# Two graph layers on one core: the run table of attention 1 as an input, its places sought ahead of the table of features, counts from the first gathered block on

## The chip, the cores and the metric

The kernel runs on one core of a Trainium2 chip. The metric is device time in microseconds; smaller is better. The program has five engines that work side by side: TensorE (PE, matrix products, with its weight loads as PEld), VectorE (DVE), ScalarE (ACT), GpSimd (POOL) and SyncE (SP, used here as a DMA queue). Each takes its instructions in the order of its own queue and waits for the others by semaphores. DMAs are issued from the queues of SP, ACT and POOL; a gather by indices (an indirect DMA) is issued from POOL.

## The reference

Two layers over a graph of 6250 nodes and 200,000 edges sorted by destination. The first is a graph attention of two rounds, the second a convolution over edges with a small network for each edge. Only the first round of attention and what it needs is touched by the change.

```python
def gat_layer(x, W, attn_l, attn_r, bias, src, dst, num_nodes):
    H, D = attn_l.shape
    feat = (x @ W).reshape(num_nodes, H, D)
    el = jnp.sum(feat * attn_l[None], axis=-1)
    er = jnp.sum(feat * attn_r[None], axis=-1)
    e = jax.nn.leaky_relu(el[src] + er[dst], NEG_SLOPE)
    m = jax.ops.segment_max(e, dst, num_segments=num_nodes)
    ee = jnp.exp(e - m[dst])
    s = jax.ops.segment_sum(ee, dst, num_segments=num_nodes)
    alpha = ee / s[dst]
    msg = feat[src] * alpha[:, :, None]
    rst = jax.ops.segment_sum(msg, dst, num_segments=num_nodes)
    return rst + bias.reshape(1, H, D)

h = jnp.maximum(_layernorm(x, axis=-1), 0.0)
h = gat_layer(h, W1, al1, ar1, b1, src, dst, N_NODES)   # 4 heads of 16
h = jax.nn.elu(h.reshape(N_NODES, -1))
h = gat_layer(h, W2, al2, ar2, b2, src, dst, N_NODES)   # 1 head of 128
x = x + h[:, 0, :]
# second layer: h = relu(layernorm(x)); messages over the edges from
# h[src], edge_attr_4 and two gelu layers of edge_attr_8; summed by dst
```

## The kernel before

The nodes are 49 blocks of 128 (`NB`); a block's edges are contiguous, since they are sorted by destination, and are read as a window of 34 tiles of 128 edges (`K`, `CAP`). The work has four stages.

**Preparation.** `x` is loaded in chunks of eight blocks by turns on the ACT and SP queues (`load_x`, L147 to L152). Both edge lists are loaded as 125 rows of 1600 (`di` and `si`, L168 to L175). From `di` come: the first edge of each block (L206 to L241, with one small indirect load `part_i`, L218), flags whether the list falls anywhere (`falls`, L201), and the low seven bits of each destination, written to `dlow` (L251 to L255). `features` in all but name is the loop at L574 to L602: layer norm statistics on VectorE (L291, L292), the normed and clipped block on ScalarE (L579), four transposes on TensorE copied out by VectorE (L312, L314), the product with the weights and attention vectors (L591), copied out by ScalarE (`t1`, L593) and VectorE (`er1`, L594); in four pieces it is written to HBM as `table1` (L597 to L600). The statistics come in two halves of 24 and 25 blocks. `node_factors` and `split3` make the factors of the destination nodes (`pq`, `pq3`), `widely` checks a spread (L441 to L452). Last, for each of 3136 half-block windows of 64 sources, ten comparisons with every 160th destination (L620) and 250 small products (L622) give the segment where its run of edges begins (`wseg`).

**Attention 1.** Two methods run side by side. Blocks 0 to 32 (`NG = NB - DENSE1` = 33) are gathered: for each of 34 tiles POOL gathers 128 rows of `table1` by source (L319, into `G`, six buffers of eight tiles), and `attend` makes weights and messages on VectorE (L324, L362 to L367), halves them (L331, L332), and sums them into nodes on TensorE (L377). `finish1` closes four blocks at a time and writes what attention 2 reads (`rhs2d`, L830). Blocks 33 to 48 are dense: `dense1` yields 128 steps (8 passes of 14 steps, a start and an end), each of which loads counts of edges between all sources and four destination blocks (L861), makes a ramp on ScalarE (L892), takes a minimum on VectorE (L895) and sums on TensorE (L902, L908); a pass ends with L915 to L943. These counts, which attention 2 needs for all 49 blocks, are made by `count` in 196 steps (four per block): VectorE compares slots with a cut list of edges (L773, twice), TensorE multiplies (L784), ScalarE copies out (L786), and a DMA on ACT's queue writes them (L788).

To cut the lists, `write_runs` writes a run table `runs` to HBM: row n holds sources and destinations of 128 edges from 16n on, as int16, in ten DMAs on ACT's queue during blocks 0 and 1. `seek_windows` finds each window's row in it: 25 indirect loads on POOL (`wpart_i`, L715), each followed by a comparison and a sum on VectorE (L720, L721). `fetch_run` gathers 128 rows of the run table (L731, 25 times) and `cut_windows` turns them into keys (L740 to L756). `fill_rhs1` turns `table1` into the dense method's right sides, seven calls (L694 to L705).

The order is written out by hand in the loop over `b` and the groups `q` (8, 8, 8, 8 and 2 tiles): each group issues its gathers and then as many counting and dense steps as are due. Counting starts at block `LAG` = 3, dense at block `LAG_D` = 7, and both are due in full with the last tile of block 32. `step` issues the second part of a step after the first part of the next. VectorE and TensorE mostly follow this order, but a planner may put an instruction ahead of others unless it is kept in program order (`keep`).

**Attention 2** begins after a branch that all engines meet at, and is dense for all blocks; **the convolution** follows. Neither is changed in its instructions.

Of the kernel before, what the change touches and what calls it, by code (L numbers as in the profile page):

```python
# [53 lines left out]
LAG = 3  # L54
AHEAD = 4
DENSE1, LAG_D = 16, 7
# [10 lines left out]
def gnn_kernel(ctx: ExitStack, tc: tile.TileContext, x, src, dst, attr4, attr8,  # L67
               W1, al1, ar1, b1, W2, al2, ar2, b2,
               Wl0, Wl1, Ws0, Ws1, Wm1, Wm2, Wtp, Wf0, Wf1, src_t, dst_t, attr4_t, attr8_t, out):
# [23 lines left out]
    NROW = (E - WCAP) // WSTEP + 1  # L93
# [11 lines left out]
    ps_bank = ps_pre.enter_context(tc.tile_pool(name="ps_bank", bufs=2, space=PSUM))  # L105

# [52 lines left out]
    fin = one.enter_context(tc.tile_pool(name="fin1", bufs=1))  # L159
    aw = one.enter_context(tc.tile_pool(name="aw", bufs=2))  # L160
# [3 lines left out]
    df = seek.enter_context(tc.tile_pool(name="df", bufs=1)).tile([GP, ROWT + 1], F32, name="df")  # L164
    listed = ExitStack()
    find = listed.enter_context(tc.tile_pool(name="find", bufs=1))
    both = []
    for name, v in (("di", dst), ("si", src)):  # L168
        t = find.tile([GP, ROWT + WCAP], I32, name=name)
        nc.vector.memset(t[:, ROWT:], NB * P)  # L170
        rows = v.rearrange("(p t) -> p t", p=GP)
        nc.sync.dma_start(t[:, :ROWT], rows)
        nc.sync.dma_start(t[:GP - 1, ROWT:], rows[1:, :WCAP])
        both.insert(0, t)

    w1_sb = const.tile([D, HD], F32, name="w1_sb")
    nc.scalar.dma_start(w1_sb, W1)
    load_x()
    w2_sb = const.tile([HD, D], F32, name="w2_sb")
    nc.scalar.dma_start(w2_sb, W2)  # L180
    a1_sb = const.tile([HD, 2 * H1], F32, name="a1_sb")
    nc.vector.memset(a1_sb, 0.0)
    for j, a in ((0, al1), (1, ar1)):
        for h in range(H1):
            nc.scalar.dma_start(a1_sb[h * DH:(h + 1) * DH, j * H1 + h:j * H1 + h + 1],
                                a[h:h + 1, :].rearrange("o d -> d o"))
    a2_sb = const.tile([D, 2], F32, name="a2_sb")
    for j, a in ((0, al2), (1, ar2)):
        nc.scalar.dma_start(a2_sb[:, j:j + 1], a.rearrange("o d -> d o"))
# [5 lines left out]
    wfirst = const.tile([P, NC], I32, name="wfirst")  # L195

    runs = dram.tile([NROW, 2, WCAP], I16, name="runs")
    di = both[1]
    nc.vector.tensor_copy(df, di[:, :ROWT + 1])
    falls = find.tile([GP, ROWT], F32, tag="row", name="falls")  # L200
    nc.vector.tensor_tensor(falls, df[:, :ROWT], df[:, 1:], op=OP.is_gt)  # L201
    fall = find.tile([GP, 1], F32, name="fall")
    nc.vector.tensor_reduce(fall, falls, axis=AX.X, op=OP.max)
    NS = ROWT // SEG
    below = find.tile([GP, NB + 1, NS], F32, name="below")
    nc.vector.tensor_tensor(below, df[:, 0:ROWT:SEG][:, None, :].to_broadcast([GP, NB + 1, NS]),  # L206
                            starts[:GP, :, None].to_broadcast([GP, NB + 1, NS]), op=OP.is_lt)
    nbelow = find.tile([GP, NB + 1], F32, name="nbelow")
    nc.vector.tensor_reduce(nbelow, below, axis=AX.X, op=OP.add)
    ps = small()  # L210
    nc.tensor.matmul(ps[:NB + 1, 0:1], nbelow, ones[:GP], start=True, stop=True)
    nc.tensor.matmul(ps[:NB + 1, 1:2], fall.to_broadcast([GP, NB + 1]), ones[:GP], start=True, stop=True)
    seg = find.tile([NB + 1, 1], F32, name="seg")
    nc.vector.tensor_scalar(seg, ps[:NB + 1, 0:1], -1.0, 0.0, op0=OP.add, op1=OP.max)
    seg_i = find.tile([NB + 1, 1], I32, name="seg_i")
    nc.vector.tensor_copy(seg_i, seg)
    part_i = find.tile([NB + 1, SEG], I32, name="part_i")
    nc.gpsimd.indirect_dma_start(  # L218
        out=part_i, out_offset=None, in_=dst.rearrange("(s t) -> s t", t=SEG),
        in_offset=bass.IndirectOffsetOnAxis(ap=seg_i[:, 0:1], axis=0))  # L220
    part = find.tile([NB + 1, SEG], F32, name="part")
    nc.vector.tensor_copy(part, part_i)
    nc.vector.tensor_scalar(part, part, own_start[:NB + 1], None, op0=OP.is_lt)
    found = find.tile([NB + 1, 2], F32, name="found")
    nc.vector.tensor_reduce(found[:, 1:2], part, axis=AX.X, op=OP.add)
    nc.vector.scalar_tensor_tensor(found[:, 0:1], seg, float(SEG), found[:, 1:2], op0=OP.mult, op1=OP.add)
    nc.vector.tensor_copy(found[:, 1:2], ps[:NB + 1, 1:2])
    pr = small()
    for j in range(2):
        nc.tensor.matmul(pr[:1, j * P:j * P + NB + 1], found[:, j:j + 1], ident[:NB + 1, :NB + 1],  # L230
                         start=True, stop=True)
    ends = find.tile([1, 2, NB + 1], F32, name="ends")
    nc.vector.tensor_copy(ends, pr[:1, :2 * P].rearrange("o (j b) -> o j b", j=2)[:, :, :NB + 1])
    first = find.tile([1, NB], F32, name="first")
    nc.vector.tensor_scalar(first, ends[:, 0, :NB], float(E - CAP), None, op0=OP.min)
    nc.vector.tensor_copy(first_i, first)
    nc.vector.tensor_sub(over, ends[:, 0, 1:], first)
    nc.vector.tensor_scalar(over, over, float(CAP), None, op0=OP.is_gt)
    nc.vector.tensor_scalar(falls_at_all, ends[:, 1, :NB], 0.5, None, op0=OP.is_gt)
    nc.vector.tensor_tensor(over, over, falls_at_all, op=OP.max)  # L240
    nc.vector.tensor_sub(n_edges, ends[:, 0, 1:], ends[:, 0, :NB])  # L241


    raws = []
    LONG = max(ROWT + WCAP, HS * 4 * P)
    for t in both:
        raw = pool.tile([P, LONG], BF16, tag="row", name="raw", bufs=3)[:GP, :ROWT + WCAP].bitcast(I16)
        nc.scalar.copy(raw, t)
        raws.append(raw)
    low_i = find.tile([GP, ROWT], I32, tag="row", name="low_i")  # L250
    nc.vector.tensor_scalar(low_i, di[:, :ROWT], P - 1, None, op0=OP.bitwise_and)  # L251
    low = find.tile([GP, ROWT], BF16, name="low")
    nc.vector.tensor_copy(low, low_i)
    dlow = dram.tile([E], BF16, name="dlow")
    nc.sync.dma_start(dlow.rearrange("(p t) -> p t", p=GP), low)  # L255
    listed.close()

    def write_runs(i, n):

        per = ROWT // WSTEP  # L260
        j, i, n = i * 2 // n, i % (n // 2), n // 2
        ends = [(GP - 1) * i // n, (GP - 1) * (i + 1) // n]
        for p0, p1, m in [(*ends, per)] + [(GP - 1, GP, NROW - (GP - 1) * per)] * (i == n - 1):
            a = raws[j][p0:p1, :]
            nc.scalar.dma_start(
                runs[p0 * per:p0 * per + (p1 - p0) * m, j, :].rearrange("(p r) t -> p r t", r=m),
                bass.AP(tensor=a.tensor, offset=a.offset, ap=[a.ap[0], [WSTEP, m], [1, WCAP]]))
# [17 lines left out]
    def shift_window(b):  # L285
        nc.vector.tensor_scalar(dstw[:, b, :], raw_dst.pop(b), -float(b * P), None, op0=OP.add)
# [368 lines left out]
    for j in range(2):  # L655
        nc.scalar.dma_start(wm1_sb[j * NRAD:(j + 1) * NRAD, j * HID:(j + 1) * HID], Wm1)
# [891 lines left out]
```

## Time and profile before

| | us |
|---|---|
| three runs, median (lowest to highest) | 4396.92 (4395.07 to 4397.64) |
| the profiled execution | 4406.11 |
| its span | 4404.4 |
| first gather of attention 1 | 112.68 |
| last gather of attention 1 | 1777.59 |
| first load of attention 2 | 1845.50 |

| engine | busy us | share of the span |
|---|---|---|
| PE | 3042.9 | 69% |
| DVE | 3565.2 | 81% |
| ACT | 2712.6 | 62% |
| POOL | 2795.3 | 63% |

All three stages differ in their limits, so a share over the whole span says little about one of them. A line of a group names source line, engine, operation and tiles (written<-read), then busy time and the mean in ns of one, then the idle time of the engine just before these instructions and what ended it. "issue" is idle time for which the profile shows no cause. [...]

### The profile page before, as it was taken

The numbers are of one execution on the slowest core, as the hardware profiler recorded it, in microseconds if no ns is written. First come the engines' busy times: TensorE is split into PE (matmuls) and PEld (weight loads), VectorE is DVE, ScalarE is ACT, GpSimd is POOL, SyncE is SP. The second block draws the span as 40 slices with busy tenths as digits, with TensorE's granted clock in tenths as the row PEclk, the third lists the DMA queues.
The fourth block names the chain that finished last, engine by engine and source line by source line (L and its number), as shares of the span: only waits on it lengthen the run. The fifth ranks groups of instructions, "written<-read, shape, count | busy, mean of one in ns | idle before, by whom it ended". The sixth has DMA issues, their size and how long they took to land. (4 is left out here: it accounts for less than half of the span.)

```text
span 4404.4 us, 61759 instructions
## 1 busy us (share of the span) xinstructions
PE 3042.9 (69%) x19255; PEld 2147.9 (49%) x19256; DVE 3565.2 (81%) x6184; ACT 2712.6 (62%) x6200; POOL 2795.3 (63%) x2752
## 2 busy tenths in 40 slices
PE   4115665666477566579998677777777777777777
PEld 3115444544355444478887344444444444444444
DVE  5258776788688688688888799999999999899998
ACT  3024556576486577689999565555555555555555
POOL 0777777777777777110000777777777777777775
PEclk9999677677677778699999788888888888888888
DMA  4346464565466556554453222222222222222221
GB/s 109 67 120 171 128 168 129 164 177 158 126 178 165 150 156 169 172 177 167 153 171 107 61 63 63 62 63 64 62 63 63 63 62 63 63 62 63 64 61 51
DMA packets 410029, 484.00 MB, mean 110 GB/s; under 512 B 248457, under 2 KB 296367, under 8 KB 405454
## 3 DMA queue, kind: packets, MB, share of 16 engines
q1 hardware_dynamic: 258854, 239.58, 18.6%
q0 software_dynamic: 87952, 149.96, 15.0%
q10 hardware_dynamic: 62872, 90.28, 5.7%
q8 instruction: 159, 2.61, 0.3%
q14 instruction: 192, 1.57, 0.1%
HBM read 369.70 MB, written 109.82 MB: 109 GB/s over the span
## 5 line engine op out<-in xcount | busy, mean ns | idle before, releaser
L319 POOL DMA_INDIRECT G<-table,srcc x1563 | 1475.1, 944 | 1003.3 <-DVE kept L1239 525.6
L319 POOL DMA_INDIRECT G<-table,srcw x1122 | 1249.0, 1113 | 417.1 <-issue 314.9
L786 ACT CAST ca<-small 128x392 bf16<-128x392 f32 x784 | 350.2, 491 | 335.9 <-PE small L784 307.0
L892 ACT ACTIVATE up<-erb,sel 128x512 bf16<-128x512 f32 x784 | 516.1, 726 | 8.6 <-DMA oht<-dlow 3.6
L1188 ACT ACTIVATE ramp<-erb,sel 128x256 bf16<-128x256 f32 (+1 forms) x1225 | 491.7, 499 | 20.7 <-DVE up L1192 14.4
L1335 PE MATMUL whole<-halves,ohr 128*128 128x512 f32 x1563 | 503.9, 461 | 0.7 <-ACT acc L1365 0.7
L1277 ACT ACTIVATE g<-G,a 128x128 f32<-128x128 f32 x1563 | 481.4, 393 | 2.0 <-DMA G<-table,srcc 0.2
L1270 PEld LDWEIGHTS big<-wtp_sb,hid 64*128 64x128 f32 x3126 | 263.6, 249 | 372.8 <-issue 358.2
L1270 PE MATMUL big<-wtp_sb,hid 64*128 64x128 f32 x3126 | 306.1, 351 | 150.2 <-DVE halves L1324 149.8
L784 PE MATMUL small<-key,lo 128*128 128x98 bf16 x3136 | 299.9, 237 | 139.6 <-ACT ca L786 109.0
L908 PE MATMUL up<-up,rc 128*102 128x512 bf16 x784 | 297.0, 539 | 142.2 <-DVE up L895 141.4
L1335 PEld LDWEIGHTS whole<-halves,ohr 128*128 128x128 f32 x1563 | 316.6, 210 | 129.5 <-issue 54.1
L377 PE MATMUL whole<-halves,ohr 128*128 128x136 f32 x1122 | 240.1, 356 | 174.6 <-DVE halves L332 138.7
L1258 PE MATMUL layer<-hid,wm_sb 128*128 128x512 f32 x392 | 341.1, 969 | 11.9 <-ACT hid L1261 11.1
L1261 ACT ACTIVATE hid<-layer 128x512 f32<-128x512 f32 x392 | 230.8, 589 | 189.6 <-PE layer L1258 189.6
L1258 PE MATMUL layer<-a8t,wm_sb 16*128 16x512 f32 x392 | 230.0, 667 | 157.2 <-ACT hid L1261 148.1
L784 PEld LDWEIGHTS <-lo 128*128 128x128 bf16 x3136 | 228.7, 115 | 209.9 <-issue 175.9
L1315 ACT CAST halves<-mess 128x512 fp32r<-128x512 f32 x195 | 114.4, 587 | 329.7 <-DVE mess L1302 329.7
L1307 DVE TENSOR_TENSOR halves<-mess,halves 128x512 fp32r<-128x512 f32 x391 | 267.8, 685 | 55.3 <-ACT halves L1310 39.8
L377 PEld LDWEIGHTS whole<-halves,ohr 128*128 128x128 f32 x1122 | 204.7, 255 | 194.7 <-DVE halves L332 137.3
L1197 PE MATMUL big<-rhs,up 128*128 128x196 bf16 x2401 | 240.5, 250 | 49.6 <-DVE up L1192 41.6
L773 DVE TENSOR_TENSOR lo<-slots,turned 128x2048 bf16<-128x2048 bf16 x196 | 238.3, 1216 | 37.4 <-PE small L784 37.2
(296 smaller groups left out, 6294.4 us busy)
## 6 DMA issues: line engine op xcount, KB each, us to landing
counts<-ca ACTq DMA_DIRECT2D x196, 392.0 KB
ct<-counts SPq DMA_DIRECT2D x192, 392.0 KB
ctc<-counts SPq DMA_DIRECT2D x896, 56.0 KB
oht<-dlow SPq DMA_DIRECT2D x33, 1088.0 KB
G<-table,srcc POOLq DMA_INDIRECT x1563
rc<-rhs SPq DMA_DIRECT2D x56, 358.8 KB
G<-table,srcw POOLq DMA_INDIRECT x1122
a8t<-attr_rows SPq DMA_DIRECT2D x391, 16.0 KB
```

Of the source, the lines that this page charges most:

```text
L319: nc.gpsimd.indirect_dma_start(out=G[:, c, :], out_offset=None, in_=table, in_offset=bass.IndirectOffsetOnAxis(ap=idx[:, c:c + 1], axis=0))
L377: nc.tensor.matmul(acc, oh[:, c, :], ms[:, c].rearrange("e s f -> e (s f)"), start=start and c == 0, stop=stop and c == n - 1)
L784: nc.tensor.matmul(ps[:, k * NKEY:(k + 1) * NKEY], lo[:, a, :, r], ky[:, a, :, r], start=True, stop=True)
L786: nc.scalar.copy(ca[:, :, i * W:(i + WBANK) * W].rearrange("p h (k d) -> p h k d", d=W), ps[:, :WBANK * NKEY].rearrange("p (k h d) -> p h ...
L892: nc.scalar.activation(up[:, i], erb[:, j], AF.Relu, bias=sel1[:, h0 + i, 2 * q + j:2 * q + j + 1], scale=STEEP)
L908: nc.tensor.matmul(sums["ups"][j][:2 * C1, :], r[:, i, c:c + 2 * C1], up[:, i], start=h0 + i == 0, stop=h0 + i == NB - 1)
L1188: nc.scalar.activation(ramp[:, h, :n * P], erb[:, :n * P], AF.Relu, bias=sel2[:, h0 + h, :], scale=STEEP)
L1258: keep(nc.tensor.matmul(ph, w, x[:, :npr * P], start=True, stop=True))
L1270: keep(nc.tensor.matmul(pw[:, c, :], hid[half, j * P:(j + 1) * P], wtp_sb[half].rearrange("x p u -> x (p u)"), start=True, stop=True))
L1277: keep(nc.scalar.activation(g0[:, c], G[:, c, :], AF.Copy, scale=a0[:, c, :]))
L1307: keep(nc.vector.tensor_tensor(ms[:, cs, 1, 1], m, ms[:, cs, 0, 1], op=OP.subtract))
L1335: keep(nc.tensor.matmul(acc, oh[:, c, :], ms[:, c].rearrange("e s h i u -> e (s h i u)"), start=start, stop=stop))
```

## The change

The run table is laid out on the host and given as an input `runs`, int32 instead of int16; `si`, its int16 copies and `write_runs` go. Small weights that were put together from many DMAs come as whole inputs (`a1_w`, `a2_w`, `lin_w`, `wm1_w`, `wm2_w`, `wtp_w`, `wf_w`), mostly on SP's queue. The preparation is written out as pieces in an order that is kept: statistics in six parts (`stats`), features in five stages per four blocks (`features`, advanced together by `through`), with the transposes copied out by ScalarE, and the searches between them. The window search (`segments`, `fetch_parts`, `count_parts`, `window_rows`) now ends ahead of the loop. The pools `fin` and `aw` are opened after the preparation's pools close. In the loop counting starts at block 0 and is due three blocks before the end (`AFTER`); dense starts at block 4 and is due 20 tiles before the end (`AFTER_D`).

```diff
-LAG = 3
-DENSE1, LAG_D = 16, 7
+DENSE1, LAG_D, AFTER, AFTER_D = 16, 4, 3, 20
...
+    def segments(i0, i1):
+        for i in range(i0, i1):
+            below = find.tile([GP, NC * P], BF16, name="belowc", bufs=2)
+            keep(nc.vector.tensor_scalar(below, wstarts, df[:, i * WSEG:i * WSEG + 1], None, op0=OP.is_gt))
+            for c in range(NC):
+                keep(nc.tensor.matmul(pcount[:, c:c + 1], below[:, c * P:(c + 1) * P], ones_b, start=i + c == 0,
+                                      stop=i == NSEG - 1 and c == NC - 1))
...
+    def fetch_parts(q):
+        part = find.tile([P, NQS, WSEG], I32, name="wpart_i", bufs=2)
+        for j in range(NQS):
+            nc.gpsimd.indirect_dma_start(
+                out=part[:, j, :], out_offset=None, in_=dst.rearrange("(s t) -> s t", t=WSEG),
+                in_offset=bass.IndirectOffsetOnAxis(ap=wseg_i[:, q * NQS + j:q * NQS + j + 1], axis=0))
+        wparts[q] = part
+
+    def count_parts(q):
+        less = find.tile([P, NQS, WSEG], F32, name="wpart")
+        cs = slice(q * NQS, (q + 1) * NQS)
+        keep(nc.vector.tensor_tensor(less, wparts.pop(q), own_w[:, cs, None].to_broadcast([P, NQS, WSEG]), op=OP.is_lt))
+        keep(nc.vector.tensor_reduce(wfound[:, cs], less, axis=AX.X, op=OP.add))
...
+    def stats(i):
+        b0, n = 8 * i, 8 if i < NB // 8 - 1 else NB - 8 * i
+        mv = pre.tile([P, n, 2], F32, name=f"mv{i}")
+        for j in range(n):
+            norm_stats(mv[:, j, :], b0 + j)
+        c = coefs(b0, n, mv)
+        next(c)
+        return c
...
+        ht = work.tile([P, 4, P], F32, name="transp")
+        keep(nc.scalar.copy(ht[:, :len(hs), :], pt[:, :len(hs), :]))
...
+    def through(k):
+        for d in range(5):
+            if 0 <= k - d < len(gens):
+                next(gens[k - d])
+
+    c0 = stats(0)
+    keep(nc.vector.tensor_copy(df, di))
+    deque(c0, 0)
+    c1 = stats(1)
+    through(0)
+    segments(0, 1)
+    through(1)
...
+    segments(6, NSEG)
+    window_segments()
+    for q in range(2):
+        fetch_parts(q)
+    c3 = stats(3)
...
+    block_segments()
...
+    block_firsts()
+    deque(c4, 0)
+    c5 = stats(5)
+    through(8)
+    count_parts(0)
+    fetch_parts(2)
+    deque(c5, 0)
+    low_parts()
+    through(9)
+    write_table(0, 24)
...
+    through(16)
+    write_table(40, NB)
     pq = pool.tile([P, NB, 2 * H1], F32, name="pq")
     node_factors(pq, er1, H1)
     split3(pre, pq3, pq, [P, NB, 2 * H1])
+    for q in range(3, 5):
+        count_parts(q)
+    window_rows()
...
+    find_falls()
+    w2_sb, a2_sb = load_weights(("w2_sb", W2), ("a2_sb", a2_w))
...
     seek.close()
+    fin = one.enter_context(tc.tile_pool(name="fin1", bufs=1))
+    aw = one.enter_context(tc.tile_pool(name="aw", bufs=2))
...
-        run = cut.tile([P, 2, WCAP], I16, name="run", bufs=2)
+        run = cut.tile([P, 2, WCAP], I32, name="run", bufs=2)
...
     for b in range(AHEAD):
         load_window(b)
+    for c in chunks[:2]:
+        fetch_run(c)
     for b in range(AHEAD):
         shift_window(b)
     low = load_low(0)
+    tables[chunks[0]] = cut_windows(chunks[0])
     for b in range(NG):
-        if b == LAG - 1:
-            deque(seeking, 0)
-        if b == LAG:
-            tables[chunks[0]] = cut_windows(chunks[0])
...
-            if b < LAG - 1:
-                for _ in range(2):
-                    next(seeking, None)
-            if b + 1 < LAG:
-                write_runs(b * len(GROUPS) + q, (LAG - 1) * len(GROUPS))
-            if b == 1 or b == 2 and q < NB // HS - len(GROUPS):
-                fill_rhs1(((b - 1) * len(GROUPS) + q) * HS, HS)
...
-            due = len(steps) * ((b - LAG) * K + s + n) // ((NG - LAG) * K)
+            if b == 0 or b == 1 and q < NB // HS - len(GROUPS):
+                fill_rhs1((b * len(GROUPS) + q) * HS, HS)
+            due = min(len(steps), len(steps) * (b * K + s + n) // ((NG - AFTER) * K))
...
-            due = n_dense * ((b - LAG_D) * K + s + n) // ((NG - LAG_D) * K)
+            due = min(n_dense, n_dense * ((b - LAG_D) * K + s + n) // ((NG - LAG_D) * K - AFTER_D))
```

## The prediction

> **What bounds the kernel now.** I read the page's slices first, to see which engine is level where.
>
> ```profile
> span 4404.4 us, 61759 instructions
> ...
> DVE  5258776788688688688888799999999999899998
> ...
> POOL 0777777777777777110000777777777777777775
> ```
>
> One slice is 110 us. GpSimd (POOL) stands at 7 from the second slice to the sixteenth without a break, while VectorE (DVE) wanders between 2 and 8. That stretch is attention 1, so I cut it into windows: before the first gather, blocks 0 to 2, blocks 3 to 6, blocks 7 to 32, and what follows the last gather. The columns are PE, PE loads, DVE, ACT and POOL busy, with instruction counts, then the granted clock, DMA share and GB/s.
>
> ```profile
> 0.00:112.70 112.70, 49.09 (x422) 39.35 (x424) 62.93 (x215) 33.33 (x79) 7.43 (x17) 1.00 0.43 109
> 112.70:274.00 161.30, 19.29 (x134) 18.14 (x134) 46.76 (x150) 8.72 (x18) 121.68 (x126) 1.00 0.32 71
> 274.00:468.00 194.00, 97.05 (x743) 84.49 (x742) 156.17 (x395) 83.32 (x185) 148.44 (x146) 0.99 0.61 167
> 468.00:1778.50 1310.50, 844.09 (x5858) 608.64 (x5859) 1012.24 (x1784) 849.59 (x1689) 1028.56 (x902) 0.72 0.58 156
> 1778.50:1845.50 67.00, 38.28 (x240) 26.87 (x239) 43.25 (x117) 39.70 (x88) 0.03 (x1) 0.66 0.27 82
> ```
>
> POOL is idle ahead of the gathers and behind them. Is its 78% in between full? The groups of POOL between 112 and 1780 us, with the idle time before each and who ended it, answer that.
>
> ```profile
> L319 POOL DMA_INDIRECT G<-table,srcw x1122 | 1249.0, 1113 | 417.1 <-issue 314.9 <-PE pe L360 65.2 <-DMA G<-table,srcw 13.7
> L731 POOL DMA_INDIRECT run<-runs,wfirst x25 | 26.1, 1043 | 7.6 <-issue 7.0 <-DVE x L696 0.3 <-DVE far L750 0.3
> L715 POOL DMA_INDIRECT wpart_i<-in_dst,wseg_i x25 | 23.6, 945 | 7.6 <-issue 7.3 <-DMA G<-table,srcw 0.3
> ```
>
> Apart from the 65.2 us ahead of the first gather, the idle time is 0.3 us of issue per instruction. The table of waits shows the only real stop:
>
> ```profile
> POOL G L319 <- DVE msg L367: 13.2, 10, 7.5
> ```
>
> So POOL's queue is the path: 1249.0 + 351.9 (417.1 less 65.2) + 33.7 + 31.2 = 1665.8 us, exactly 112.7 to 1778.5. In that stretch the other engines matter only where they stop POOL. A gather takes 0.944 us undisturbed, 1.113 on average; the timeline shows what stretches it.
>
> ```profile
> 803.26 2.01 DVE L895 TENSOR_TENSOR up<-up,ctc 128x3584 bf16<-128x3584 bf16 x1
> 803.94 2.15 POOL L319 DMA_INDIRECT G<-table,srcw  x1 [0.30 <-issue]
> ...
> 809.78 1.23 DVE L773 TENSOR_TENSOR lo<-slots,turned 128x2048 bf16<-128x2048 bf16 x1 [0.46 <-PE small L784]
> 810.32 0.94 POOL L319 DMA_INDIRECT G<-table,srcw  x1 [0.31 <-issue]
> ```
>
> The dense minimum (L895, both operands in SBUF) holds a gather; the counting compare (L773, one operand in PSUM) does not. The start and the end of the stretch:
>
> ```profile
> 110.89 0.82 DVE L340 TENSOR_TENSOR pq<-rest,pq 128x392 bf16<-128x392 f32 x1
> ...
> 112.68 0.96 POOL L319 DMA_INDIRECT G<-table,srcw  x1 [65.17 <-PE pe L360]
> ...
> 1777.59 0.94 POOL L319 DMA_INDIRECT G<-table,srcw  x1 [0.30 <-issue]
> ...
> 1788.42 0.69 DVE L367 TENSOR_TENSOR msg<-G,msg 128x512 f32<-128x512 f32 x1
> ...
> 1820.69 0.23 DVE L990 TENSOR_TENSOR sums<-sums,whole 128x68 f32<-128x68 f32 x1 [3.76 <-ACT sums L989]
> ...
> 1841.04 0.70 DVE L829 TENSOR_TENSOR rr<-x,rr 128x520 bf16<-128x520 f32 x1
> ...
> 1845.50 0.34 ACTq L1169 DMA_DIRECT2D ct<-counts  x1
> ```
>
> The first gather starts when VectorE has finished its preparation; 67 us after the last one attention 2 begins. Lastly, VectorE's groups between 112 and 275 us: it sits idle behind the window search, in order, while counting hasn't begun.
>
> ```profile
> L720 DVE TENSOR_SCALAR wpart<-wpart_i,own_w 128x160 f32<-128x160 int32 x25 | 7.9, 315 | 63.3 <-DMA wpart_i<-in_dst,wseg_i 63.2
> ```
>
> **What the Trainium skill says.** *SBUF — State Buffer*, "Who interferes with whom": a VectorE instruction with two SBUF inputs contends with a GpSimd instruction that reads SBUF, and one in a two-port mode with any GpSimd instruction; the loser blocks. The trace agrees (2.15 us beside L895, 0.94 beside L773), although the page infers that descriptor generation escapes `tensor_tensor`. *DMA: Bandwidth & Descriptors*, "Anatomy of one DMA — SWDGE (gpsimd) path", gives about 2 us fixed from issue to completion; here the search of block starts (L218) was issued at 34.5 and used at 41.4, so I take 7 us. *ScalarE: Activation LUTs*, "What ACT_TABLE_LOAD costs", gives 1283 ns, as the trace's three loads do; since all square roots still precede the first exponential, I add none.
>
> **The change part by part**, against the profiled execution (span 4404.4, 4406.1 with what lies around it; the runs' median is 4396.9, 9 us less, and I carry the difference over to it).
>
> *1. The search leaves the gathers' queue.* 25 L715 instructions, 23.6 + 7.6 = 31.2 us, go to the prologue, where POOL is busy 7.4 of 112.7 us. There they are five groups of 25 × 1.25 / 5 = 6.2 us, hidden beside features. The two first run fetches also move ahead of the first gather: 2.5 us. Gain 33.7.
>
> *2. Dense steps come under the gathers.* Five L895 (of 112) ran after the last gather before; now dense ends 20 tiles ahead of it. By 1249.0 − 1122 × 0.944 = 190 us of stretching over some 140 holding instructions (107 L895, 31 one-hots L350) each costs 1.3: loss 6.5. Counting is free of it. So the loop takes 1665.8 − 33.7 + 6.5 = 1638.6.
>
> *3. Counts and fills from block 0.* They only matter if VectorE stops POOL. In blocks 0 and 1 VectorE needs per block five groups of about 3.3, a one-hot 1.4, 6.5 counts of 2.18 and 1 for cutting, 33 us; the seven `fill_rhs1` calls, at 14.7 + 14.1 + 10.6 + 10.1 = 49.5 from L694, L705, L703 and L696, fall there too. Two blocks: 66 + 49.5 = 116 us, while POOL takes 68 × 1.3 = 88. VectorE falls 28 us behind, with the first one-hot's load (now started late) perhaps 40; six G buffers hold 48 gathers, 60 us. No stop, so zero; the cost if that cover fails is up to 20. Later blocks need nothing new: the rate is still one thirtieth of the counts per block, and dense is thinner.
>
> *4. The tail.* Now 67 us pass: VectorE is two to three groups late, works off counts and dense, and the last dense pass needs 27 us from its last sums to L829. Afterwards counts are over three blocks early and dense 20 tiles, some 25 us, early, so that chain ends about when the last block does: landing and two groups about 8, `finish1` of one block 6.5 (1820.4 to 1827), flags and barrier about 7. I take 22; bounds 17 and 37. Gain 45.
>
> *5. The first gather.* VectorE's 62.9 us before it lose the evictions that go to ScalarE (L314, 8.8), one-hots (3.5 + 2.7), a cast and memsets (2.5); they gain five grouped window counts (800 elements at the rate of L201 and L203, 1.8 each: 9.0), four more coefficient pairs (1.9), and statistics without overlap because the order is pinned (6): 62. `si`'s 781 KB, the run table's writes and the small weight loads leave the early queues; x came at 21.3, I take 16. Preparation up to the last coefficients is 62 − 17 − 3 = 42 us, with 8 of hand-offs: 66. About six matmul groups at 3.0 remain: 84. The table lands 8 later, 92. VectorE's closing work is factors and split 3.6, two counts 3.6, places 0.7, `widely` 2.5, falls 4.6, weights 2: 17, so 101. Prologue memory and gather buffers overlay each other, hence I take the later one, 102 against 112.7: gain 10.7. If memory comes free with the table it is 92; if each hand-off stalls the pinned order, 118.
>
> *6. The rest costs nothing:* weights as seven plain loads on SP (VectorE may wait 5 us for `wtp_sb`, beside gathers); int32 runs (128 KB a fetch; two operations of 0.2 us a chunk); the falls' search, merely moved. Attention 2 and the convolution keep their instructions.
>
> Sum: −10.7 − 27.2 − 45 = −82.9. Span 4321.5; median 4396.9 − 82.9 = 4314.0.
>
> **The rivals.** *B, VectorE stops POOL early and keeps a tail:* for it, VectorE at 156 of 194 us when fills and counts met; against, only 7.5 us of longest stop there or later. Start 112, loop 1638.6 + 20, tail 37: −0.7 − 7.2 − 30 = −38, so 4359. *C, a short prologue:* nothing waits on the closing work, hand-offs overlap, start 88; tail 17; the fewer DMAs remove the 12 us of POOL waits: −24.7 − 39 − 50 = −114, so 4283. *D, slower:* the pinned order prevents overlap in the features. A round runs serially on ScalarE (four times 0.48), PE (0.9), ScalarE (0.7), PE (2.0) and ScalarE (0.4), with five hand-offs near 0.2: 7 us, thirteen rounds 91, plus 16 for x and 62 of VectorE plus 27 of stops: 196. That is +83 against −72 from loop and tail, 4408; it decides from a start at 185. Against: the five-stage interleaving of `through` puts different blocks side by side. That the change doesn't do what it says would show as window fetches after the first gather; the code excludes it.
>
> **How the numbers follow.** Forecast 0.63, B 0.18, C 0.12, D 0.07. The range, 4285 to 4355, takes the forecast's bounds and most of C and some of B. This kernel's measurement separates about 0.2%, 8.8 us; of D I leave 0.02 within it and 0.05 above. Faster 0.93, same 0.02, slower 0.05.
>
> **What would show it.** First gather near 102; no window fetch after it; 1122 gathers in about 1639 us with a mean still near 1.11; attention 2's first load about 22 us behind the last gather, near 1763; after that 2559 us as now. Wrong if POOL waits on `msg` by tens of us in the first four blocks, if the first gather waits beyond 118, or if dense closes the stage more than 37 us behind the last gather.

## The result, and the profile after

The changed kernel takes 4352.87 us, the median of four runs (4348.14 to 4354.85); the kernel before took 4397.28 us in four (4395.07 to 4398.40). The ratio is 0.9898, with a 95% interval of 0.9881 to 0.9915: 44.4 us less, where 82.9 were forecast. The time lies inside the stated range of 4285 to 4355, at its upper edge.

The page first: its span, and the slices of VectorE and GpSimd.

```profile
span 4351.2 us, 61730 instructions
...
DVE  5877686976897785588886999899988999899898
...
POOL 3777777777777777100001777777777777777775
```

GpSimd is level at 7 in slices 2 to 16, as before, and the first slice, 0 before, is 3: the window fetches lie there now. VectorE's second and third slice, 2 and 5 before, are 8 and 7: counting begins with the first block. The same stretches as before, cut at this kernel's own marks: preparation, from the first gather to the end of the last, from there to attention 2's first load, attention 2, and the rest (columns as in the prediction's windows).

```profile
0.00:113.90 113.90, 41.22 (x412) 37.36 (x413) 61.32 (x202) 36.19 (x92) 35.29 (x41) 0.95 0.35 80
113.90:1746.60 1632.70, 968.26 (x6933) 720.29 (x6933) 1232.37 (x2304) 975.21 (x1956) 1283.32 (x1147) 0.70 0.56 153
1746.60:1785.80 39.20, 12.63 (x56) 10.51 (x56) 19.24 (x101) 6.91 (x22) 0.04 (x1) 0.50 0.17 42
1785.80:2340.00 554.20, 483.71 (x5074) 439.15 (x5074) 465.80 (x812) 529.01 (x1352) 13.76 (x1) 0.97 0.50 171
2340.00:4351.20 2011.20, 1517.41 (x6778) 933.95 (x6778) 1778.96 (x2716) 1170.91 (x2792) 1477.53 (x1563) 0.83 0.23 61
```

| us | before | forecast | after |
|---|---|---|---|
| first gather | 112.7 | 102 | 113.9 |
| first gather to the end of the last | 1665.8 | 1638.6 | 1632.7 |
| from there to attention 2's first load | 67.0 | 22 | 39.2 |
| the rest | 2558.9 | 2558.9 | 2565.4 |
| span | 4404.4 | 4321.5 | 4351.2 |

The loop came out 5.9 us below its forecast. The start didn't become shorter at all, and the tail shrank by 28 us instead of 45. Each has its own place in the trace. GpSimd's groups up to 1900 us, then its waits:

```profile
L346 POOL DMA_INDIRECT G<-table,srcw x1122 | 1256.5, 1120 | 348.2 <-issue 312.5 <-DMA G<-table,srcw 16.8 <-PE small L713 6.4
L223 POOL DMA_INDIRECT wpart_i<-in_dst,wseg_i x25 | 28.6, 1142 | 71.3 <-DVE bnst L318 42.2 <-DVE wpart L231 17.5 <-issue 6.4
L781 POOL DMA_INDIRECT run<-runs,wfirst x25 | 26.9, 1076 | 7.6 <-issue 5.2 <-DVE w L391 0.6 <-DVE hi L798 0.3
```

```profile
POOL wpart_i L223 <- DVE wpart L231: 17.5, 1, 17.5
...
POOL G L346 <- DVE msg L394: 1.8, 6, 0.3
```

The 25 window fetches (L223) are out of the loop. What is left of it adds up: 1256.5 + (348.2 − 6.4) + 26.9 + 7.6 = 1632.8 us. No gather waits for VectorE longer than 0.3 us. But ahead of the loop the fetches stop once for 17.5 us, since a third group needs a buffer that a count (L231) must first free.

The start, from the timeline:

```profile
15.45 0.29 DVE L318 BATCH_NORM_STATS2 bnst<-xt 128x6 f32<-128x128 f32 x1 [4.95 <-DMA xt<-in_x]
...
23.61 0.43 SPq L176 DMA_DIRECT2D wtp_sb<-wtp_w  x1
25.72 0.21 DVE L739 TENSOR_SCALAR wtp_sb<-wtp_sb 128x96 f32<-128x96 f32 x1 [6.05 <-DMA wtp_sb<-wtp_w]
25.93 0.20 DVE L590 RECIPROCAL scale<-sd 128x8 f32<-128x8 f32 x1
...
43.98 3.03 DVE L206 TENSOR_SCALAR belowc<-wstarts,df 125x3200 bf16<-125x3200 int16 x3 [3.59 <-PE pcount L208]
...
54.15 0.17 DVE L629 COPY er<-small 128x16 f32<-128x16 f32 x1 [2.66 <-ACT t L628]
...
83.50 0.17 DVE L592 SCALAR_TENSOR_TENSOR bias<-mv,scale 128x9 f32<-128x9 f32 x1
...
100.32 0.16 DVE L629 COPY er<-small 128x4 f32<-128x4 f32 x1 [0.17 <-ACT t L628]
...
113.40 0.38 PE L713 MATMUL small<-a_sb,w2t 128*64 128x2 f32 x2 [1.65 <-DVE w2t L711]
...
113.92 0.94 POOL L346 DMA_INDIRECT G<-table,srcw  x1 [6.43 <-PE small L713]
```

`x` is there at 15.45 us. But the last weights, used in the convolution over two milliseconds later, are scaled (L739) before the first reciprocal of the statistics (L590), and VectorE stands 6.05 us for their load, which SP issued only at 23.61. In the code this scaling is marked with `keep` and stands behind the whole preparation (L739; the last call for features, `through(16)`, is above it): that it ran ahead is the planner's doing, and `keep` did not prevent it. Why the planner put it there isn't shown. The last coefficients of the statistics come at 83.7 (L592), the features end at 100.3, and the closing work, with the second layer's product (L713) last, lets the first gather go at 113.92.

The tail, from the timeline (SPq is SP's DMA queue):

```profile
1745.70 0.94 POOL L346 DMA_INDIRECT G<-table,srcw  x1 [0.30 <-issue]
...
1767.06 2.31 SPq L880 DMA_DIRECT2D rhs2d<-rr  x2
1768.93 0.43 DVE L313 TENSOR_SCALAR dstw<-dsti 128x34 f32<-128x34 int32 x4
1769.60 0.97 SPq L310 DMA_DIRECT2D dsti<-in_dst  x1
1771.07 0.35 SPq L308 DMA_DIRECT2D srcw<-in_src  x1
1771.64 0.33 SPq L310 DMA_DIRECT2D dsti<-in_dst  x1
1771.90 0.18 DVE L313 TENSOR_SCALAR dstw<-dsti 128x34 f32<-128x34 int32 x1 [2.54 <-DMA dsti<-in_dst]
...
1782.16 0.33 SPq L310 DMA_DIRECT2D dsti<-in_dst  x1
1783.74 0.36 DVE L313 TENSOR_SCALAR dstw<-dsti 128x34 f32<-128x34 int32 x3 [3.81 <-DVEq L503]
...
1785.85 0.34 ACTq L1209 DMA_DIRECT2D ct<-counts  x1
```

The last results (L880) are issued between 1767.06 and 1769.4. After that SP loads, a pair every 1.4 us, the edge windows of the last dense blocks (L308, L310), and VectorE shifts them (L313); nothing reads these tiles for blocks 33 to 48. The change marked L313 with `keep`; in the kernel before the shift was free, and the last of these loads was issued at 1774.86, ahead of the last gather.

### The profile page after: what moved, and what is told of

It reads as the page before. It is cut to its first block, busy times and chain, and to the rows that moved or that the text cites. A ratio compares the mean times of both kernels' runs of the same rounds, so it can differ in the third digit from the quotient of the medians.

```text
span 4351.2 us, 61730 instructions
## 1 busy us (share of the span) xinstructions
PE 3023.2 (69%) x19253; PEld 2141.3 (49%) x19254; DVE 3557.7 (82%) x6130; ACT 2718.2 (62%) x6213; POOL 2809.9 (65%) x2752
## 5 line engine op out<-in xcount | busy, mean ns | idle before, releaser
L346 POOL DMA_INDIRECT G<-table,srcw x1122 | 1256.5, 1120 | 348.2 <-issue 312.5
L1373 PEld LDWEIGHTS whole<-halves,ohr 128*128 128x128 f32 x1563 | 318.7, 211 | 131.7 <-issue 56.2
L391 DVE TENSOR_TENSOR w<-w,G 128x64 f32<-128x64 f32 (+1 forms) x165 | 34.8, 211 | 291.6 <-DMA G<-table,srcw 239.3
```

The source lines that it names most:

```text
L346: nc.gpsimd.indirect_dma_start(out=G[:, c, :], out_offset=None, in_=table, in_offset=bass.IndirectOffsetOnAxis(ap=idx[:, c:c + 1], axis=0))
L1373: keep(nc.tensor.matmul(acc, oh[:, c, :], ms[:, c].rearrange("e s h i u -> e (s h i u)"), start=start, stop=stop))
```

## The experiments

The theory after this reading: **A**, two instructions that the change marked with `keep` (L739 at the start, L313 in the tail) cost about 6 and 13 us, and the rest of the start is the closing work ahead of the first gather. **B**, what these waits hide is as long as they are, so taking one away changes little.

On the chips of these runs the loop and the convolution took longer (loops of about 1950 to 2075 us, the kernel before 5408 to 5533 us in the median), with the waits on TensorE's results longer and often without a releaser in the trace, and the totals scatter by 1 to 3%; start, tail and attention 2 of the changed kernel kept their lengths. So start and tail are compared, from the profiles, and the totals say little. The changed kernel, run there again, shows this:

> The changed kernel itself, taken again beside the other run on the same chip, as what it is compared with: first gather at 113 to 115, tail 39 to 42; where the whole of the kernel before takes about 4397 us, ratio 0.988 to 0.992 to it. On a chip where the loop is longer, the start and the tail are still these.

```profile
0.00:114.10 114.10, 43.30 (x412) 39.57 (x413) 61.35 (x201) 36.29 (x92) 35.47 (x41) 1.00 0.35 80
114.10:2122.90 2008.80, 985.51 (x6933) 727.40 (x6933) 1236.62 (x2304) 987.22 (x1956) 1240.04 (x1147) 0.72 0.46 124
2122.90:2162.90 40.00, 12.85 (x56) 10.56 (x56) 19.43 (x102) 6.91 (x22) 0.00 (x1) 0.50 0.17 41
2162.90:2717.00 554.10, 484.63 (x5074) 439.91 (x5074) 465.45 (x809) 528.58 (x1351) 13.73 (x1) 0.97 0.50 171
```

```profile
POOL G L346 <- DVE msg L394: 206.2, 32, 14.3
```

Start 114.1, tail 40.0 and attention 2 at 554.1 us, against 113.9, 39.2 and 554.2; the loop differs, and the convolution behind it. In this loop the gathers do wait for VectorE, behind `msg` alone for 206.2 us, where it was 1.8: GpSimd's queue is no longer all of the path, so that work taken off it need not shorten the loop. The ratio to the kernel before was 0.9966 (0.9932 to 0.9999); 0.988 to 0.992 were expected for a chip on which the kernel before takes 4397 us. What a kernel gains in all doesn't carry over to such a chip.

**The tail: no window loads for the dense blocks, and the shift free to move.**

```diff
-        if b + AHEAD < NB:
+        if b + AHEAD < NG:
             load_window(b + AHEAD)
-        if b:
+        if b and b + AHEAD - 1 < NG:
             shift_window(b + AHEAD - 1)
...
-    for b in range(NG + AHEAD - 1, NB):
...
```

> The changed kernel without the edge windows of blocks 33 to 48, which no gather reads (nothing of the result is left out). Theory A (the 39 us behind the last gather end with these loads on the SP queue, which the pinned order put last): first load of attention 2 some 24 to 27 us behind the last gather, the kernel 12 to 15 us faster than the changed kernel (about 4339). Theory B (the end of the last dense pass and the branch set the tail): still 36 to 40 us, the same time within 3 us.

The loads and shifts for blocks 33 to 48 are left out here. The tail was 32.0 us, shorter than theory B's 36 to 40 but longer than A's 24 to 27, the first gather at 114.1; ratio 0.9809 (0.9761 to 0.9857). Two waits, 3.8 us on VectorE and 8.6 us on TensorE's weight loads, have no releaser in the trace; they end 3.3 and 3.7 us into this tail.

```diff
-        keep(nc.vector.tensor_scalar(dstw[:, b, :], raw_dst.pop(b), -float(b * P), None, op0=OP.add))
+        nc.vector.tensor_scalar(dstw[:, b, :], raw_dst.pop(b), -float(b * P), None, op0=OP.add)
```

> Only the shift of an edge window (L313) is taken out of the order that is held to the program's; the loads of the dense blocks' windows stay. Theory A (the hold pushes the last window loads behind the last VectorE work, and they stand at the end of the tail): the loads go back under the gathers, the tail from the end of the last gather to attention 2's first load falls from 39 to 25 to 32 us, as in the run that leaves these loads out (32), and the time falls by 7 to 14 us. Theory B (the loads are late for a reason of their own, such as the order of SP's queue): tail 37 to 41, time unchanged within 3 us. First gather stays at 113 to 115 in both.

The windows of this kernel:

```profile
113.10:2121.30 2008.20, 977.55 (x6933) 724.62 (x6933) 1239.99 (x2311) 986.14 (x1955) 1246.16 (x1147) 0.66 0.44 124
2121.30:2147.90 26.60, 10.76 (x49) 8.82 (x49) 17.91 (x91) 7.35 (x23) 0.01 (x1) 0.50 0.16 49
```

The tail is 26.6 us with every load still made: the last window load is issued at 2111.4, ahead of the last gather, instead of 13 us after the last result. So the hold costs 12.6 to 13.4 us of the tail, and the loads cost the tail nothing when they lie under gathers. Theory A holds for the tail; ratio 0.9939 (0.9904 to 0.9974).

**The start: the scaling of the last weights behind attention 2.**

```diff
-    keep(nc.vector.tensor_scalar(wtp_sb[:, 0:3, :], wtp_sb[:, 0:3, :], 1.0 / math.sqrt(HID), None, op0=OP.mult))
-    keep(nc.vector.tensor_scalar(wtp_sb[:, 3, :], wtp_sb[:, 3, :], 1.0 / math.sqrt(3.0 * HID), None, op0=OP.mult))
...
+    keep(nc.vector.tensor_scalar(wtp_sb[:, 0:3, :], wtp_sb[:, 0:3, :], 1.0 / math.sqrt(HID), None, op0=OP.mult))
+    keep(nc.vector.tensor_scalar(wtp_sb[:, 3, :], wtp_sb[:, 3, :], 1.0 / math.sqrt(3.0 * HID), None, op0=OP.mult))
     wo_sb = cw.tile([4 * MUL, 2, D], F32, name="wo_sb", bufs=1)
```

> The changed kernel with the two scalings of the convolution's weights moved behind attention 2. Theory A (VectorE stopped 6 us for these weights ahead of the first coefficients, and its serial chain carries this to the first gather): first gather near 108, kernel 5 to 6 us faster than the changed kernel (about 4347). Theory B (the arrival of x or the features' hand-offs set the start, the stop is slack): first gather still 112 to 114, same time within 2 us.

```profile
19.85 0.20 DVE L590 RECIPROCAL scale<-sd 128x8 f32<-128x8 f32 x1 [0.32 <-ACT sd L587]
...
107.43 0.94 POOL L346 DMA_INDIRECT G<-table,srcw  x1 [5.33 <-PE small L713]
```

The reciprocal comes 6.1 us earlier and so do the features (94.2 against 100.3); the first gather at 107.43 gains 6.5. All of the wait reached the end of the preparation, as theory A says. Ratio 0.9885 (0.9844 to 0.9925); the 5 to 6 us that A expected of the whole can't be read from it.

**The start: the closing work.** The test for falling indices goes behind `low_parts`, the second layer's product behind the end of the preparation.

```diff
     low_parts()
+    find_falls()
...
-    find_falls()
     w2_sb, a2_sb = load_weights(("w2_sb", W2), ("a2_sb", a2_w))
-    pw = small()
...
     ps_pre.close()
...
+    pw = small()
```

> The changed kernel with the search for falls moved from the end of the preparation into a stretch where VectorE sat idle, and the product of attention 2's weights moved behind the preparation. Theory A (the first gather waited 6.4 us for this closing work, since gather buffers overlay the preparation's memory): first gather at 108 to 111, 3 to 6 us faster (about 4348). Theory B (the last window fetch of POOL, which ended at 107.5, and its count set the start in any case): first gather at 112 to 114, same time within 2 us.

```profile
19.55 0.20 DVE L590 RECIPROCAL scale<-sd 128x8 f32<-128x8 f32 x1
...
99.68 0.39 ACT L628 COPY t<-small 128x272 f32<-128x272 f32 x1 [2.95 <-remote]
...
109.18 0.20 DVE L739 TENSOR_SCALAR wtp_sb<-wtp_sb 128x96 f32<-128x96 f32 x1
...
111.20 0.94 POOL L346 DMA_INDIRECT G<-table,srcw  x1 [11.42 <-DVE wfound L235]
```

The first gather came at 111.2, 2.7 earlier than in the changed kernel, but this isn't the closing work's doing. In this run the planner put the scaling of the last weights at 109.18, so the wait for them is gone here too: the first reciprocal is at 19.55. This run is therefore to be compared with the scaling alone, and against its 107.4 the first gather is 3.8 later. From the end of the features to the first gather it is 9.1 us instead of 13.2, and what ends the wait is now the last window count; but the features end at 102.1 instead of 94.2. Of these 7.9 us, 4.7 are two waits of ScalarE whose releaser the trace doesn't show (2.95 and 1.78 us); why the features are later is open. Ratio 0.9861 (0.9823 to 0.9899). So neither theory was tested, and no gain from moving the closing work is shown.

**The input alone, in the kernel before.** `runs` comes as an input (int16), `write_runs` and `si` go, nothing else.

```diff
-    for name, v in (("di", dst), ("si", src)):
+    for name, v in (("di", dst),):
...
-    runs = dram.tile([NROW, 2, WCAP], I16, name="runs")
...
-            if b + 1 < LAG:
-                write_runs(b * len(GROUPS) + q, (LAG - 1) * len(GROUPS))
```

> The kernel before, with the run table as an input and nothing else of the change: its 20 writes and the copy of the source list are left out. Theory A (the table's writes lay under other work): the time stays within 3 us of before, first gather 110 to 113, loop within 5 us of 1666. Theory B (the writes took transfer time from the first blocks' gathers, or ScalarE's queue): the loop is 8 to 15 us shorter.

Before, then this kernel:

```profile
21.32 0.49 DVE L291 BATCH_NORM_STATS2 bnst<-xt 128x6 f32<-128x128 f32 x2 [13.45 <-DMA xt<-in_x]
```

```profile
15.39 0.49 DVE L274 BATCH_NORM_STATS2 bnst<-xt 128x6 f32<-128x128 f32 x2 [7.33 <-DMA xt<-in_x]
...
106.39 0.96 POOL L302 DMA_INDIRECT G<-table,srcw  x1 [64.30 <-DVE w L345]
```

The first gather came at 106.4, 6.3 earlier than the 112.7 of before and outside what theory A gave: `x` is 5.9 us earlier, as SP no longer loads the source list ahead of it. The tail was 86.3 us, where it is 67.0 in the first profile of before: since the input is all that differs in the code, a tail with the old due times seems longer on such a chip. What the writes cost the loop can't be read here; the ratio, 0.9973 (0.9933 to 1.0012), doesn't tell it from no change. So the changed kernel's start is, in three runs: 112.7, less 6.3 for the input (106.4), plus 1.0 for all else of the change when the scaling is away (107.4), plus 6.5 for the scaling (113.9).

**The due times.** LAG and LAG_D of before (3 and 7), fills in blocks 1 and 2, all steps due with the last tile; the rest as changed. Run twice.

```diff
-            due = min(len(steps), len(steps) * (b * K + s + n) // ((NG - AFTER) * K))
+            due = len(steps) * ((b - LAG) * K + s + n) // ((NG - LAG) * K)
...
-            due = min(n_dense, n_dense * ((b - LAG_D) * K + s + n) // ((NG - LAG_D) * K - AFTER_D))
+            due = n_dense * ((b - LAG_D) * K + s + n) // ((NG - LAG_D) * K)
```

> The changed kernel with the old dues: fills in blocks 1 and 2, counts from block 3, dense from block 7, both due with the last tile. Search ahead of the table and run table as an input stay. Theory A (dues are worth the tail alone: 67 us before, 39 after; the gathers take as long as before less the search): loop 1626 to 1636 us, tail 60 to 70 us, kernel 20 to 32 us slower than the changed kernel (about 4379). Theory B (starting early also slowed or sped the gathers by tens of us): loop off by more than 10 us from 1633.

> The changed kernel with the due times of before (counts from block 3, dense steps from block 7, ends at the last tile), taken again. Theory A (the new due times only move the dense steps from the tail to under the gathers and bring the gathers no delay of note): the tail is 95 to 105 us against 39, the loop 5 to 15 us shorter than the changed kernel's 1633, the sum 45 to 60 us slower than the changed kernel. Theory B (work under the gathers costs them as much as it saves): loop 35 us or more shorter, the sum within 15 us of the changed kernel.

The tail of the first and of the second run:

```profile
2117.30:2217.20 99.90, 53.48 (x336) 38.07 (x335) 63.04 (x152) 56.52 (x120) 0.01 (x1) 0.64 0.29 87
```

```profile
2064.30:2161.90 97.60, 52.68 (x328) 37.48 (x327) 59.65 (x149) 53.16 (x114) 0.00 (x0) 0.64 0.29 85
```

VectorE has 60 to 63 us of work left when the last gather ends, against 19 in the changed kernel: the new due times take about 58 to 60 us off the tail here, on chips where that of before is longer too (86.3). The first run's expectation of 60 to 70 us was a miss; the second's was set after it. Of the loops, 2003.2 us lies among the others on these chips (2001 to 2075) and 1950.2 below them all. Loop and tail together are 2103.1 and 2047.8 us, against 2048.8 in the changed kernel, one execution each: the first fits theory A of the second text, the second theory B. The ratios, 0.9887 (0.9854 to 0.9920) and 0.9997 (0.9952 to 1.0043), don't agree either, so what the due times bring in all is open on these chips. What is shown is that with the old ones VectorE's work is left for the tail.

**Towards a better version.** The scaling, the closing work and the dense windows together:

> Three edits together: the two scalings of the last weights behind attention 2, the test for falling indices and the second layer's product out of the way of the first gather, and no window loads for the dense blocks. If the three add up: first gather at 104 to 106 against 113.9, tail 25 to 32 against 39, together 15 to 22 us less than the changed kernel. If one wait hides another (the window fetches on the gathers' own queue end at 107 whatever is cleared away): first gather 107 to 110, together 8 to 14 us less.

```profile
100.14 0.39 ACT L628 COPY t<-small 128x272 f32<-128x272 f32 x1 [4.37 <-remote]
...
111.62 0.95 POOL L346 DMA_INDIRECT G<-table,srcw  x1 [11.29 <-DVE wfound L235]
```

First gather at 111.6, later than with the scaling alone and outside both expectations; tail 31.4, as expected. The start is that of the closing-work run (111.2), whose edit is in it: the features ended at 102.5 instead of 94.2, again behind waits of ScalarE whose releaser the trace doesn't show (4.37 us here). So the three don't add up in this run: with the closing work's edit in it, some 4 us of the scaling's gain are lost again, and why is open. Total 5387.2 beside 5450.9, without an interval.

Then all five groups of window fetches at once, each with its own buffer, so that none waits for a count:

```diff
-        part = find.tile([P, NQS, WSEG], I32, name="wpart_i", bufs=2)
+        part = find.tile([P, NQS, WSEG], I32, name="wpart_i", bufs=NC // NQS)
...
-    for q in range(2):
+    for q in range(5):
         fetch_parts(q)
```

> The changed kernel with what the runs so far point to: the shift of a window free to move, the two scalings behind attention 2, the test for falling indices early and the second layer's product late, and all five window fetches issued together into buffers of their own, so that no fetch waits for a count. Theory A (the start is set by VectorE's waits and by the fetches that wait for counts): the last window fetch ends near 80, the features at 94 to 95, the first gather at 99 to 104 against 113.9; the tail 25 to 32 against 39; together 17 to 29 us less than the changed kernel, ratio to the kernel before 0.983 to 0.986 where the whole takes 4397. Theory B (the features' own chain of hand-offs and the memory that the gathers' buffers share with the preparation set the start): first gather 105 to 109, together 11 to 16 us less than the changed kernel.

GpSimd, then VectorE, of this kernel:

```profile
76.72 0.94 POOL L256 DMA_INDIRECT part_i<-in_dst,seg_i  x1 [0.30 <-issue]
```

```profile
79.05 0.18 DVE L262 CAST part<-part_i 50x40 f32<-50x40 int32 x1 [12.93 <-DMA part_i<-in_dst,seg_i]
```

Neither theory came true. The fetches did run to 76 us without a stop, but the one fetch for the blocks' first edges (L256) stood behind all 25, and VectorE stopped 12.93 us for it, with the last statistics behind that. The features were late, and the first gather came at 119.6, 5.7 later than in the changed kernel; the tail, with the shift free, was 26.5. Ratio 0.9849 (0.9772 to 0.9926). Next, the same with three of the five groups written behind that fetch:

> The five-buffer version again, with the one fetch for the blocks' first edges between the second and the third group of window fetches instead of behind all 25. Theory A (the last run lost its gain only because VectorE stood waiting for that one fetch, queued behind 25 others): VectorE doesn't stop before the last group's statistics, features end at 93 to 96, first gather 100 to 105, tail 25 to 30; together 20 to 28 us less than the changed kernel. Theory B (more than that one fetch holds the features): first gather 107 or later, together 8 to 18 us less.

```profile
76.35 0.95 POOL L256 DMA_INDIRECT part_i<-in_dst,seg_i  x1 [0.31 <-issue]
```

The planner put the 25 fetches ahead of it all the same (none of them is marked with `keep`); the start is 118.4, and the theories stay untested. Ratio 0.9917 (0.9890 to 0.9945). Last, the shift free, the scaling and the closing work together, with the fetches as they were:

> The three edits that each worked by themselves (the window's shift free, the two scalings behind attention 2, the falls test early and the second layer's product late), with the window fetches as in the changed kernel. If they add up: first gather 104 to 107, tail 25 to 30, together 17 to 23 us less than the changed kernel. If one hides another: first gather 107 to 111, together 12 to 17 us less.

```profile
0.00:107.70 107.70, 39.33 (x412) 35.62 (x413) 62.58 (x203) 36.15 (x92) 34.46 (x41) 0.93 0.36 85
...
2166.70:2194.10 27.40, 10.96 (x48) 8.87 (x48) 17.92 (x91) 7.35 (x23) 0.00 (x0) 0.50 0.15 48
```

Start 107.7 and tail 27.4: against 114.1 and 40.0 of the changed kernel on such a chip, 6.4 + 12.6 = 19.0 us less. The sum is as expected if they add up, the start isn't (104 to 107): the scaling alone gave 107.4, so the closing work adds nothing. The features ended 2.3 us later than there (96.5), and from their end to the first gather it is 11.2 us against 13.2. The ratio is 0.9879 (0.9834 to 0.9925); the changed kernel didn't run on this chip, so a gain in the whole time over it isn't shown.

## Why the prediction came out as it did

The sign and the loop's term were right and the size was not: 38.9 us are missing from the forecast of 4314.0. Against the profiled execution of before, the start is 11.9 us worse than forecast, the loop 5.9 better, the tail 17.2 worse, the rest 6.5 worse, together 29.7. The other 9.2 are the difference between that execution (4406.1) and the median of the runs (4396.9): it was carried over to the changed kernel, whose own profiled execution had none of it.

- **Step 1, the search off the queue: right.** The 31.2 us of L715 are gone from the loop. The two first run fetches did not move ahead of the first gather: two gathers went first, and the fetches came at 116.4 and 117.7. So 2.5 of the 33.7 weren't won, and with the run fetches a little slower the loop holds 34.5 us of them where 31.2 were left in the sum. No run moves the search alone: that the loop's gain is the search's rests on this sum of GpSimd's queue.
- **Step 2, dense steps under the gathers: right in kind, the size partly by luck.** The gathers' busy time grew from 1249.0 to 1256.5, by 7.5 where 6.5 were forecast. By their overlap in the two traces, an estimate, 148 of the 190 us beyond 0.944 us a gather lay beside dense minima (L895, now L945) before and 151 of 197 after, so about half of the growth is theirs. That most of it lies there agrees with the Trainium skill's *SBUF — State Buffer*, "Who interferes with whom", on VectorE instructions with two SBUF inputs.
- **Step 3, no stop of GpSimd: right.** The waits on `msg` fell from 13.2 to 1.8 us. This was a gain that the forecast left out: idle time before gathers, without the first, fell from 351.9 to 341.8. The loop is thus shorter than forecast through 10.1 us not foreseen, less 1.0 and 3.3 on the other side from steps 2 and 1.
- **Step 4, the tail: the mechanism right, the size wrong.** The due times do what was said: the results of the last dense pass and of the last gathered block go out together, between 1767.1 and 1769.4, and with the old ones the tail was 98 to 100 us on the other chips. The terms that failed are two. To the last results 8 + 6.5 = 14.5 us were taken, and it was 22.7 (1746.6 to 1769.4). And "flags and barrier about 7" held nothing for the window loads, though the change puts `keep` around the shift: they take 12.6 to 13.4 us, with some 3.4 left for flags and barrier. With the shift free 26.6 are left against 22, within the bounds of 17 and 37. The 39.2 is beyond the 37 that was named as a sign of being wrong, but what closes the stage is these loads, which stand behind the last dense results.
- **Step 5, the first gather: wrong.** `x` was taken at 16 and came at 15.45, and the closing work took 13.6 us where 17 were taken. The features failed: "84" was the end forecast for them, and it was 100.3. The six matmul groups took about 17 where 18 were taken; it is the last coefficients, forecast for 66, that came at 83.7. Of these 17.7 us, 6.1 are one wait for the last weights, as its removal shows. Step 6 had priced that very wait, at "5 us for `wtp_sb`, beside gathers", where the code has it; it ran ahead of the first coefficients, where nothing covers it. The other stops of VectorE up to there are 18.0 us where 8 were taken for hand-offs: five on ScalarE's copy (L628), 12.2 us together, 4.8 on the window sums (L208) and 1.0 on small products. VectorE's own work is the rest, about 44 where 42 were taken. Which of the stops could be avoided was not settled.
- **Step 6, the rest: nothing shown against it.** Attention 2 is the same (554.5 and 554.2). What follows took 6.8 us longer in one execution; its instructions are the same, and why it differs is open.

Rival B's time, 4359, lies nearer to the result than the forecast, and its tail of 37 nearly came (39.2). Its mechanism did not, on the chip that was forecast for: no gather of the loop waited for VectorE longer than 0.3 us. On the other chips such waits did come, also in the kernel with the old due times. Rival C's short start needed a prologue in which nothing waits; rival D's features in series did not come either, with 113.9 against the 185 from which it decides.

## What to carry to other kernels

When a change pins an order, look up in the trace where every pinned instruction landed, and write beside it the load that it waits for and when that load is issued: here two instructions that the stage doesn't need cost 6 and 13 us, and one of them ran far ahead of its place in the code. When an edit's gain is read, look first whether the planner moved something else with it. When a queue that bounds a loop gets shorter, the engines beside it don't: their work must begin earlier, or it is left for the tail. And before more requests are put ahead on a queue, look for the one small request behind them that somebody waits for.

## What the runs showed of the hardware

- Indirect fetches on GpSimd kept a pace of 1.25 us, 17 in a row (55.5 to 75.5 us in the run with five buffers), and the one put behind them was used 2.3 us after its start, 1.4 us after its own line on GpSimd had ended: the 12.9 us of VectorE were the queue, not the transfer. In the kernel before the same load was used 6.9 us after its start, which the prediction took over; why it took longer there isn't shown.
- Pairs of small window loads on SP went at 1.4 us a pair (eight pairs from 1771.07 on, with one step of 2.2 us among them), in a stretch where little else was under way.
- On other chips the loop's VectorE and TensorE work was as long (1236.6 and 985.5 us against 1232.4 and 968.3) and the gathers' shorter (1240.0 of GpSimd against 1283.3), yet the loop took 2008.8 us instead of 1632.7. The granted clock doesn't explain it (0.72 and 0.70); many of the waits there have no releaser in the trace, and what ended them is open.
